# A macaron block on one core: square sums ahead of the splits, a second load queue, and a tile's feed-forward network in the opening stage

## The chip, the cores and the metric

The kernel runs on one NeuronCore of a Trainium2 chip. Five engines work side by side, each in the order of its own instruction list: TensorE (PE; PEld is its weight load), VectorE (DVE), ScalarE (ACT), GpSimd (POOL) and SyncE (SP). DMAs are issued by SP and by ACT, each on its own queue. The metric is the device time of one execution in microseconds (us); lower is better.

## The reference

Two batches of 1024 tokens with 1024 features pass through half a feed-forward network, attention, and the same half feed-forward network again:

```python
def ffn(x):                                   # x: layer norm of the stream
    top2 = softmax over the two largest of x @ gate_w.T       # 8 experts
    low  = x @ lora_A[e].T                    # 16 per expert, 128 together
    return x @ base_w.T + base_b + 2 * sum_e top2[e] * (low[e] @ lora_B[e].T)

def attn(x):                                  # 32 heads of 32, 8 k/v heads
    q, k, v = x @ Wq, x @ Wk, x @ Wv;  q, k = rope(q), rope(k)
    return (softmax(causal(q k^T / sqrt(32))) @ v) @ Wo

x = x + 0.5 * ffn(layernorm(x))
x = x + attn(layernorm(x))
x = x + 0.5 * ffn(layernorm(x))
```

All inputs are fp32.

## The kernel before

**Numbers.** Every fp32 operand of a dense product is kept as a high and a low fp16 part, and a product is three matmuls: high by high, high by low, low by high (`dense`, L362 to L364). Weights must be scaled by a power of two before they are split. `pow2` finds it: ACT squares the whole chunk and adds it up per partition (L170; the squared values themselves go to a place nobody reads, called junk), TensorE spreads the sums over the partitions (L175), POOL takes the square root (L178), and DVE and POOL make the scale and its inverse. `split` then makes both parts of one 128x512 piece: high on ACT (L195) or, for every fourth piece, on POOL (L193), low on DVE (L196).

**Weights.** The gate and lora_A (`prep_gate`), lora_B (`prep_lora`) and the two column blocks of the base matrix (`prep_base`, b0 and b1, eight splits each) stay in SBUF. The attention matrices go as five chunks (2: k and v; 0 and 1: the halves of q; 3 and 4: the halves of the output matrix, called o0 and o1 here) through `prep_stream`: two staged halves are squared, split into two fp16 tiles and written to DRAM (`wstr`), from where the `ws` tiles are later reloaded. Chunks 2, 0 and 1 are also used directly from `ws`. In `prep_stream` junk is the very fp16 tile that the splits then fill, so squares can start only when that tile is free. Staging slots are reused, so a chunk's load is issued when the one before it in the slot has been split.

**Tiles.** Tokens go in 16 tiles of 128. For each: `stage_a1` (layer norm, first ffn in three parts, layer norm again), `stage_a2` (k and v, then both halves of q, rope), attention, `stage_c1` (output matrix), `stage_c2` (second ffn). A layer norm ends with a DMA transpose on SP (`Split.add`, hl to tt, L318). In `ffn` the matmuls of gate and lora_A (24, 128x136) come first, then the two bias adds on POOL (L399), a dozen small operations that pick the experts, and the two halves of 24 matmuls with the three of lora_B each (L444 to L446), added to the stream by DVE (L447).

**The opening.** Up to the first attention unit the order is written by hand: loads on SP, gate, lora_B, b0, b1, then the loop over `START`, in which each entry advances `stage_a1` of that tile by one part and `prep_rest`, the generator of the five chunks, in step; an "f" advances `first_a2`, which runs tiles 0 and 1 together through k/v and q. A scheduler then reorders within the engines by dependences and its own timeline, except where instructions are pinned. The line is

```python
    START = (0, 0, 1, 1, 0, 1, 2, 2, 2, "f", "f", "f", "f", "f", "f")
```

**Attention.** A unit is a tile and a k/v head. L571 makes scores (with a mask matmul, L576), DVE takes the row maximum (L588), writes it beside q, and SP transposes q again (L554); L686 makes scores against that, ACT takes the exponential (L692), POOL masks the diagonal (L694), and L633 multiplies with v. `step(s)` runs the units of tile s and mixes in the dense work that `plan(s)` names; step 0 takes the three parts of tile 3's and of tile 4's `stage_a1`.

Of the kernel before, what the change touches and what calls it, by code (L numbers as in the profile page):

```python
# [9 lines left out]
FP = mybir.dt.float32  # L10
# [29 lines left out]
def kernel(  # L40
# [26 lines left out]
    tp = ctx.enter_context(tc.tile_pool(name="tp", bufs=4))  # L67
# [9 lines left out]
    vp = ctx.enter_context(tc.tile_pool(name="va", bufs=TPB + 1))  # L77
# [31 lines left out]
    kts = stat.tile([P, TPB + 1, NKV, P], HP)  # L109
    wss = [stat.tile([P, 2, KB // 2, 512], HP, name=f"ws{j}") for j in range(3)]  # L110
# [31 lines left out]
    stg = stage_ctx.enter_context(tc.tile_pool(name="stg", bufs=1))  # L142

# [22 lines left out]
    def pow2(aps, junk, name, least=None):  # L166

        am = small.tile([P, 2], FP, name="am")
        for j, (ap, jk) in enumerate(zip(aps, junk)):
            nc.scalar.activation(jk, ap, AF.Square, accum_out=am[:, j : j + 1])  # L170
        sq = small.tile([P, 1], FP, name="sq")
# [6 lines left out]
        nc.gpsimd.tensor_tensor(ar, ar, half, ALU.pow)  # L178
# [11 lines left out]

    def split(hi, lo, src, s, k):
        if k % 4 == 3:
            nc.gpsimd.tensor_scalar(hi, src, s, 0.0, ALU.mult, ALU.add)  # L193
        else:
            nc.scalar.activation(hi, src, AF.Copy, scale=s)  # L195
        nc.vector.scalar_tensor_tensor(lo, src, s, hi, ALU.mult, ALU.subtract)  # L196

    def prep_base(n, sts):
# [6 lines left out]
        pow2(sts, [wb[:, n, 0, h * HK : (h + 1) * HK, :] for h in range(2)], ("b", n), least)  # L205
# [11 lines left out]
    def prep_gate(sts):  # L217
        pow2(sts, [ag[:, 0, h * HK : (h + 1) * HK, :] for h in range(2)], ("a",))
# [7 lines left out]
    def prep_lora(st):  # L226
# [7 lines left out]
        nc.scalar.mul(bb, bb, 0.5)  # L234
# [15 lines left out]
    kth = kth.rearrange("p (a k n) -> p a k n", a=2, n=512)  # L250

    def prep_stream(ci, slots, after, keep):

        parts = CHUNKS[ci][1]
        sts = [staged.pop((ci, h)) for h in range(2)]
        sps = []
        for h in range(2):
            sps.append(wss[slots[h]] if slots[h] < 3 else kth)
            if h == 0:
                for name, c0, c1 in parts:  # L260
                    pow2([st[:, :, c0:c1] for st in sts], [sps[0][:, j, :, c0:c1] for j in range(2)], name)
                    yield
            sp = sps[h]
            for k in range(HK):
                for name, c0, c1 in parts:
                    split(sp[:, 0, k, c0:c1], sp[:, 1, k, c0:c1], sts[h][:, k, c0:c1], S[name], k)
                yield
# [7 lines left out]
    def prep_rest():  # L275
        yield from prep_stream(2, (0, 1), [(1, 0, 0), (1, 1, 1)], True)
        yield from prep_stream(3, (2, 3), [(4, 0, 2), (4, 1, 5)], False)
        yield from prep_stream(0, (2, 0), [None, None], True)
        for j in range(2):
            nc.gpsimd.memset(qst[j][:, :, 3 * DH :], 0.0)  # L280
        yield from prep_stream(1, (1, 2), [None, None], True)
        yield from prep_stream(4, (0, 1), [None, None], False)
# [49 lines left out]
    def layernorm(xt, act=False, n=1):  # L332
# [18 lines left out]
        for i in range(n):  # L351
            c = bass.ts(i, D // n)
            nc.scalar.activation(xn[:, c], xt[:, c], AF.Identity, bias=nb, scale=rs)
# [40 lines left out]
    def ffn(xt, tt, done):  # L394
        psa = p_misc.tile([P, 512], FP, name="misc")
        yield from dense(psa[:, 0 : P + E], tt, lambda k: (ag[:, 0, k, :], ag[:, 1, k, :]))
        for n in range(2):
            c = bass.ts(n, 512)
            nc.gpsimd.tensor_tensor(xt[:, c], xt[:, c], bb[:, c], ALU.add)  # L399
# [26 lines left out]
        yield True  # L426
        psb = [None, None]
# [63 lines left out]
    def kv_out(t, ps):  # L491
        i = t % TPB
        k1 = rope(ps[:, 0:256], 256, NKV, i)
        va = vp.tile([P, NKV, DH], FP, name="va")
# [247 lines left out]


# [15 lines left out]
    a1 = [stage_a1(t) for t in range(3)]  # L759
    next(a1[0])  # L760
    prep_gate(gst)
    pow2([lst[:, bass.ts(h, 512)] for h in range(2)], [lbh[:, bass.ts(h, 512)] for h in range(2)], ("l",))
    b1 = [piece(3 + h, [wb_in[:, 512:1024]], h, nc.sync) for h in range(2)]
    prep_base(0, b0)
    load_x(2)
    next(a1[1])
# [240 lines left out]
```

## Time and profile before

| | |
|---|---|
| median of 3 runs | 1524.11 us (1524.08 to 1530.86) |
| the profiled execution | 1522.65 us |
| its span | 1520.9 us |
| busy: PE, DVE, ACT, POOL | 94%, 70%, 45%, 33% |
| PE busy in the first 152 us | 102.61 us |
| first L686 (start of attention) | 151.96 us |
| DMA | 267.57 MB, mean 176 GB/s |

The page gives busy time per engine and, in 40 equal slices, the busy share in tenths. Matmul ends are modelled, so busy time of PE is not PE at its peak. Lines of the timeline read: start, duration, engine, line, operation, output<-input, count, and in brackets how long the engine had been idle and what ended it. PEclk is the clock granted to TensorE as a share of full speed.

### The profile page before, as it was taken

How to read it: one execution, taken by the hardware profiler on the slowest of the kernel's cores; microseconds unless marked ns; L12 is line 12 of the kernel's file. 1: busy time of each engine (PE TensorE's matmuls, PEld its weight loads, DVE VectorE, ACT ScalarE, POOL GpSimd, SP SyncE). 2: the span in 40 equal slices, each digit the busy share in tenths (PEclk: the TensorE clock that was granted, in tenths of full speed). 3: DMA queues.
4: the chain of work that ended last, by engine and by line, in shares of the span. 5: the costliest groups of instructions: out<-in, count | busy, mean ns of one | idle time of the engine just before them, and what ended most of it. 6: DMA issues, size and time to landing. Idle time of an engine off the chain costs nothing.

```text
span 1520.9 us, 39480 instructions
## 1 busy us (share of the span) xinstructions
PE 1428.8 (94%) x16596; PEld 832.9 (55%) x16596; DVE 1067.4 (70%) x2396; ACT 691.1 (45%) x1280; POOL 496.6 (33%) x711
## 2 busy tenths in 40 slices
PE   3877989899999999999999998999999999999998
PEld 1433445556656566666654454555556566566543
DVE  6978666867768577776663757867777577776653
ACT  7444333544444454454550334444444455565521
POOL 3453342624324133232131423434333132231231
PEclk9998999999999999999999999999999999999999
DMA  9966796957484753646546769668594652663461
GB/s 280 298 195 208 162 276 185 227 152 235 94 249 97 210 173 77 232 118 150 185 119 243 184 163 254 184 183 224 92 269 86 203 169 75 210 143 78 123 190 43
DMA packets 297186, 267.57 MB, mean 176 GB/s; under 512 B 262576, under 2 KB 265648, under 8 KB 276528
## 3 DMA queue, kind: packets, MB, share of 16 engines
q1 hardware_dynamic: 293456, 252.47, 61.4%
q10 hardware_dynamic: 3552, 12.58, 2.2%
q8 instruction: 130, 2.13, 0.6%
q14 instruction: 48, 0.39, 0.1%
HBM read 181.63 MB, written 20.45 MB: 133 GB/s over the span
## 4 chain that ended last, share of the span: by engine, by line
PE 74%; DVE 10%; DMA 8%; issue 2%; POOL 2%; ACT 1%; SPq 1%; DVEq 0%; POOLq 0%; ACTq 0%
PE av L633 15%; PE pd L362 13%; PE pd L363 13%; PE pd L364 13%; PE s L571 8%; PE s L686 7%; DMA ws<-wstr 3%; DMA qt<-qst 3%; DVE ws L196 1%; DVE mx L588 1%; DVE hl L315 1%; DMA tt<-hl 1%; PE pd L444 1%; PE pd L446 1%; PE pd L445 1%
## 5 line engine op out<-in xcount | busy, mean ns | idle before, releaser
L692 ACT ACTIVATE p<-s,cs 128x512 f32<-128x512 f32 x576 | 379.0, 687 | 277.9 <-PE s L686 274.7
L588 DVE TENSOR_REDUCE mx<-s 128x4 f32<-128x512 f32 x480 | 315.8, 675 | 161.7 <-PE s L571 148.7
L633 PE MATMUL av<-p,va 128*32 128x128 f32 x4608 | 236.9, 277 | 1.7 <-POOL p L694 1.0
L362 PE MATMUL pd<-ws,tt 128*128 128x512 f16 x592 | 226.2, 382 | 10.1 <-DMA ws<-wstr 6.3
L633 PE MATMUL av<-p,ones 128*32 128x128 f32 x4608 | 232.2, 273 | 0.0
L363 PE MATMUL pd<-ws,tt 128*128 128x512 f16 x592 | 225.9, 382 | 0.0
L364 PE MATMUL pd<-ws,tt 128*128 128x512 f16 x592 | 225.4, 382 | 0.0
L571 PE MATMUL s<-kts,qt 96*128 96x128 f16 x2304 | 200.0, 220 | 14.1 <-DMA qt<-qst 9.1
L686 PE MATMUL s<-qt,kts 128*128 128x512 f16 x576 | 201.0, 381 | 9.0 <-DMA qt<-qst 6.8
L362 PEld LDWEIGHTS <-tt 128*128 128x128 f16 x1360 | 133.9, 99 | 136.3 <-DMA tt<-hl 13.0
L363 PEld LDWEIGHTS <-tt 128*128 128x128 f16 x1360 | 133.9, 98 | 132.1 <-issue 15.2
L571 PEld LDWEIGHTS <-qt 96*128 96x128 f16 x2304 | 151.4, 98 | 98.3 <-issue 35.7
L364 PEld LDWEIGHTS <-tt 128*128 128x128 f16 x1360 | 134.0, 99 | 127.8 <-issue 6.5
L362 PE MATMUL pd<-wb,tt 128*128 128x512 f16 x512 | 196.0, 383 | 7.7 <-DMA tt<-hl 3.7
L363 PE MATMUL pd<-wb,tt 128*128 128x512 f16 x512 | 195.5, 382 | 1.0 <-DVE wb L196 1.0
L364 PE MATMUL pd<-wb,tt 128*128 128x512 f16 x512 | 195.3, 381 | 0.0
L633 PEld LDWEIGHTS av<-p,va 128*32 128x32 f32 x4608 | 122.5, 110 | 68.6 <-issue 59.4
L642 DVE RECIPROCAL rc<-o 128x128 f32<-128x128 f32 x128 | 121.0, 945 | 49.8 <-ACT o L640 49.6
L649 POOL TENSOR_TENSOR tt<-o,tt 128x128 f16<-128x128 f32 x128 | 55.5, 434 | 295.6 <-ACT tt L648 295.5
L694 POOL TENSOR_SCALAR_AFFINE_SELECT p<-p 128x512 f32<-128x512 f32 x128 | 84.3, 659 | 200.9 <-ACT p L692 200.9
L633 PEld LDWEIGHTS av<-p,ones 128*32 128x32 f32 x4608 | 138.3, 110 | 0.1
L583 POOL TENSOR_SCALAR_AFFINE_SELECT sm<-sm 128x512 f32<-128x512 f32 x96 | 62.1, 647 | 204.2 <-ACT sm L582 203.9
(175 smaller groups left out, 1796.0 us busy)
## 6 DMA issues: line engine op xcount, KB each, us to landing
ws<-wstr SPq DMA_DIRECT2D x148, 1024.0 KB, 5.6
wstr<-ws ACTq DMA_DIRECT2D x9, 1024.0 KB, 5.6
xt<-in_x_dram SPq DMA_DIRECT2D x16, 512.0 KB, 4.2
out_dram<-xt SPq DMA_DIRECT2D x15, 512.0 KB, 2.9
qt<-qst SPq DMA_TRANSPOSE x256, 3.2
ws<-in_wb_dram SPq DMA_DIRECT2D x2, 1024.0 KB, 8.3
qst<-in_wb_dram SPq DMA_DIRECT2D x2, 1024.0 KB, 7.3
st<-in_wo_dram SPq DMA_DIRECT2D x2, 1024.0 KB, 10.0
```

The costliest lines, as they stand in the source:

```text
L362: nc.tensor.matmul(ps, lhsT=th, rhs=wh, start=(k == 0), stop=False)
L363: nc.tensor.matmul(ps, lhsT=th, rhs=wl, start=False, stop=False)
L364: nc.tensor.matmul(ps, lhsT=tl, rhs=wh, start=False, stop=(last and k == KB - 1))
L571: nc.tensor.matmul(ps[:, h, :], lhsT=q[0 : 3 * DH, h, :], rhs=KT[b0 + j][0 : 3 * DH, g, :], start=(not pem or h == 0), stop=not pem,)
L583: nc.gpsimd.affine_select(out=sm, in_=sm, compare_op=ALU.is_ge, fill=-3.0e38, base=0, pattern=[[0, GRP], [-1, P]], channel_multiplier=1,)
L588: nc.vector.tensor_reduce(mx[:, j, :], ps, AX.X, ALU.max)
L633: prev = nc.tensor.matmul(av[rows, i, :], lhsT=w, rhs=p32[:, h, :], start=(us[0][0] == 0 and n == 0 and i == 0), stop=(us[-1][0] == L - 1 ...
L642: nc.vector.reciprocal(rc, o[:, 1, :])
L649: nc.gpsimd.tensor_tensor(c.low(g), o2, c.high(g), ALU.subtract)
L686: ins = nc.tensor.matmul(ps.rearrange("p h k -> p (h k)"), lhsT=KT[b0 + j][:, g, :], rhs=q.rearrange("p h k -> p (h k)"), start=True, stop ...
L692: nc.scalar.activation(p32, ps, AF.Exp, scale=cs)
L694: nc.gpsimd.affine_select(out=p32, in_=p32, compare_op=ALU.is_ge, fill=0.0, base=0, pattern=[[0, GRP], [1, P]], channel_multiplier=-1,)
```

## The change

Six things, all in the opening or in what it touches:

- Squares and the rest of `pow2` are separate. `stream_squares` squares the next chunk into a junk tile of its own after the second step of the current chunk's first half, and not ahead of the last ACT split of b1. `base_squares` and the gate's squares are called apart from `pow2` likewise: b0's squares are named before those of lora_B.
- b1 and the k/v chunk are loaded through ACT's queue, behind tile 0's normalised copy (`xn`); before, b1 went through SP's queue and k/v through ACT's, later.
- The bias is loaded and halved earlier, and the two bias adds of a tile move behind the expert choice and behind the last `pow2` power on POOL.
- `START` runs tile 0 and then tile 1, and takes tile 3's three parts between the "f" entries; step 0 keeps tile 4's only. Tile 4's input load moves there too.
- The v tiles become one tile `vas` with ten places (nine before); the last eight hold the first half of o0 during the opening, so o0 no longer goes through `ws` tile 2.
- The pool of tt tiles has five buffers (four before).

```diff
-    tp = ctx.enter_context(tc.tile_pool(name="tp", bufs=4))
+    tp = ctx.enter_context(tc.tile_pool(name="tp", bufs=5))
-    vp = ctx.enter_context(tc.tile_pool(name="va", bufs=TPB + 1))
+    vas = stat.tile([P, TPB + 2, NKV, DH], FP)
+    junk = stg.tile([P, 1, HK, 512], HP, name="junk").to_broadcast([P, 2, HK, 512])
-    def pow2(aps, junk, name, least=None):
+    def squares(aps, junk):
         am = small.tile([P, 2], FP, name="am")
         for j, (ap, jk) in enumerate(zip(aps, junk)):
             nc.scalar.activation(jk, ap, AF.Square, accum_out=am[:, j : j + 1])
+        return am
+    def pow2(am, name, least=None):
...
-        nc.gpsimd.tensor_tensor(ar, ar, half, ALU.pow)
+        marks["pow"] = nc.gpsimd.tensor_tensor(ar, ar, half, ALU.pow)
...
+    def stream_squares(ci):
+        if (ci, 0) not in staged or (ci, 1) not in staged or ci in sums:
+            return
+        sts = [staged[ci, h] for h in range(2)]
+        with tc.issue_after(marks["b1"].ins):
+            sums[ci] = [
+                squares([st[:, :, c0:c1] for st in sts], [junk[:, j, :, 0 : c1 - c0] for j in range(2)])
+                for _, c0, c1 in CHUNKS[ci][1]
+            ]
-    def prep_stream(ci, slots, after, keep):
+    def prep_stream(ci, slots, after, keep, nxt):
...
+                if k == 1 and nxt is not None:
+                    stream_squares(nxt)
...
-        yield from prep_stream(3, (2, 3), [(4, 0, 2), (4, 1, 5)], False)
+        yield from prep_stream(3, (4, 3), [(4, 0, 2), (4, 1, 5)], False, 0)
...
     def ffn(xt, tt, done):
-        for n in range(2):
-            c = bass.ts(n, 512)
-            nc.gpsimd.tensor_tensor(xt[:, c], xt[:, c], bb[:, c], ALU.add)
...
         yield True
+        with tc.issue_after(marks["pow"].ins):
+            for n in range(2):
+                c = bass.ts(n, 512)
+                nc.gpsimd.tensor_tensor(xt[:, c], xt[:, c], bb[:, c], ALU.add)
...
-    a1 = [stage_a1(t) for t in range(3)]
+    a1 = [stage_a1(t) for t in range(4)]
     next(a1[0])
+    with tc.issue_after(marks["xn"].ins):
+        b1 = [piece(3 + h, [wb_in[:, 512:1024]], h, nc.scalar) for h in range(2)]
+        stage(2, 0, 0, nc.scalar)
+        stage(2, 1, 1, nc.scalar)
     prep_gate(gst)
-    pow2([lst[:, bass.ts(h, 512)] for h in range(2)], [lbh[:, bass.ts(h, 512)] for h in range(2)], ("l",))
-    b1 = [piece(3 + h, [wb_in[:, 512:1024]], h, nc.sync) for h in range(2)]
-    prep_base(0, b0)
+    am = base_squares(0, b0)
+    pow2(squares([lst[:, bass.ts(h, 512)] for h in range(2)], [lbh[:, bass.ts(h, 512)] for h in range(2)]), ("l",))
+    prep_base(0, b0, am)
+    marks["b0"] = marks[2]
     load_x(2)
-    next(a1[1])
     pin(nc.sync.dma_start(out=bb, in_=bias_in.partition_broadcast(P)))
-    stage(2, 0, 0, nc.scalar)
-    stage(2, 1, 1, nc.scalar)
-    prep_base(1, b1)
+    nc.scalar.mul(bb, bb, 0.5)
+    for _ in chunk(a1[0]):
+        pass
+    with tc.issue_after(marks["b0"].ins):
+        am = base_squares(1, b1)
+    next(a1[1])
+    prep_base(1, b1, am)
+    marks["b1"] = marks[6]
...
     load_x(3)
+    load_x(4)
...
-    START = (0, 0, 1, 1, 0, 1, 2, 2, 2, "f", "f", "f", "f", "f", "f")
+    START = (0, 0, 1, 1, 1, 2, 2, 2, "f", "f", 3, "f", 3, "f", 3, "f", "f")
...
         if s == 0:
-            return [("a1", 3)] * 3 + [("a1", 4)] * 3
+            return [("a1", 4)] * 3
```

## The prediction, before the changed kernel ran

> **What bounds the kernel now.** I read the busy slices of the page first, then busy time by stretch, then the list of TensorE's instructions with the idle time before each, then the same list of the other engines up to the first attention unit.
>
> ```profile
> PE   3877989899999999999999998999999999999998
> PEclk9998999999999999999999999999999999999999
> ```
>
> ```profile
> 0.00:152.00 152.00, 102.61 (x511) 50.32 (x512) 119.15 (x293) 82.69 (x130) 66.96 (x101) 0.91 0.80 245
> 152.00:180.00 28.00, 27.25 (x211) 13.06 (x210) 19.61 (x53) 10.37 (x22) 10.20 (x18) 1.00 0.64 174
> 180.00:260.00 80.00, 71.04 (x698) 37.50 (x702) 52.59 (x128) 29.90 (x63) 24.62 (x39) 0.98 0.84 213
> 260.00:500.00 240.00, 233.69 (x2847) 140.26 (x2836) 182.69 (x404) 113.18 (x216) 90.12 (x125) 0.99 0.68 177
> ```
>
> Columns: stretch, its length, busy time (instructions) of PE, PEld, DVE, ACT, POOL, then granted clock, DMA share, GB/s. TensorE is the bound from the first attention unit on (27.25 of 28 us, 233.69 of 240). Only the first four slices have holes: 49.4 us of the first 152 are idle (152 - 102.61), at a mean clock of 0.91. That is the stage the change rewrites.
>
> ```profile
> 35.97 0.61 PE L362 MATMUL pd<-wb,tt 128*128 128x512 f16 x1 [3.67 <-DMA tt<-hl]
> 85.90 0.80 PE L175 MATMUL s<-ident,sq 128*128 128x128 f32 x2 [6.25 <-DVE sq L173]
> 110.02 0.38 PE L542 MATMUL pd<-ws,tt 128*128 128x512 f16 x1 [2.79 <-ACT va L495]
> 124.24 0.79 PE L175 MATMUL s<-ident,sq 128*128 128x128 f32 x2 [8.13 <-DVE sq L173]
> 151.96 0.38 PE L686 MATMUL s<-qt,kts 128*128 128x512 f16 x1 [0.61 <-DMA qt<-qst]
> ```
>
> The two longest holes stand before L175, the matmul that spreads a chunk's sum of squares: TensorE works in order, and that matmul waits for squares that come late. The last line is the first L686, the start of attention for tile 0; I use it as the clock of this stage: 151.96.
>
> ```profile
> 79.17 1.90 ACT L170 ACTIVATE ws<-qst 128x2048 f16<-128x2048 f32 x1
> 89.27 1.93 ACT L195 ACTIVATE ws<-qst,s_q 128x512 f16<-128x512 f32 x3
> 41.76 8.77 POOL L399 TENSOR_TENSOR xt<-xt,bb 128x512 f32<-128x512 f32 x6 [4.03 <-ACT bb L234]
> 23.36 2.61 ACTq L158 DMA_DIRECT2D st<-in_wv_dram  x1
> 17.68 1.53 SPq L158 DMA_DIRECT2D qst<-in_wb_dram  x2
> ```
>
> Squares of the first q chunk start at 79.17 (behind tile 2's lh, 77.86) and its splits only at 89.27. POOL's six bias adds (1.46 us each) hold back the k and v power until 50.5. The second base block is issued at 17.68, after tile 0's transpose. The fourth DMA that ACT issues in a row takes 2.61 us.
>
> **The change part by part.** Counts do not change: the same squares, splits, bias adds, matmuls. So the sum is a sum of shifts, read from the two instruction orders with the durations above.
>
> *b1 and k/v loads on ACT's queue.* They now stand behind tile 0's xn and hl and ahead of the gate splits (11.20 before). xn ends near 10.15 (its nb is ready at 8.9). Six issues follow: the trace has 0.44, 0.86, 0.54 and 2.61 for the four k/v loads (512 KB each), and b1's two of 1 MB come ahead of them; the sixth also waits until the second half of b0 has landed (issued 4.8, median 8.3 to landing: 13.1). Free again at 13.7 if nothing is held, at 19.8 if three issues cost 2.61; I take two, 17.3, as the 2.61 row is the nearest. Gate splits +6.1. The squares of lora_B (1.25 us) now lie between b0's squares: +1.25. b0's splits start near 28.5 (21.3).
>
> Against that, b1 (2 MB) is there early. The Trainium skill ("DMA: Bandwidth & Descriptors", section "Issuing engines are not separate DMA queues") speaks against this part: DMAs of all issuing engines interleave on the same 16 engines, and only the sequencer's issue time is saved. The trace shows DMA nearly idle (share 0.06) from 14.25 to 16.5, before tile 0's transpose moves, so the gain would be an earlier start and not bandwidth. By the rule b0's rest is slowed while both queues run, which the 13.7 to 19.8 contains. By this trace the early b1 is worth nothing in the sum: b1's squares must wait for ACT's b0 splits (28.5 + 3.9), as they did before.
>
> *b1's splits.* Squares end at 36.5. POOL's power stands behind tile 2's hl, and DVE's tile 0 add behind two bias adds (2.9): splits at 46.6 to 52.8, before 35.2 to 44.0. +9.
>
> *Bias adds in pairs behind the power; squares ahead.* The power of k and v no longer waits behind 8.8 us of adds. ACT after b1's splits (46.6 + 6 x 0.63 = 50.4, less waiting than DVE): lora_B's part is done by 51, though k/v's four squares (1.15 each) end near 54, o0's two (2.0 each) near 57.5, half of q0's near 59.6, since all of them stand ahead of the k/v splits. These then run on DVE 59.6 to 66.3 (16 of 0.39 and small ones; before 53.9 to 62.3): +4. DVE goes on when q0's second square is in (66.7): eight o0 splits of 0.66, tile 1's two adds 1.4, one hl 1.2, two statistics 1.2, about 14 small ones 2.3: 78 (72.4). q0's first half then needs no new square: small ones 1.5, four splits with two small ones 3.2: 79 to 83, where it was 90.0 to 94.7. This is where the change pays: 11 us.
>
> *The a2 stage of tiles 0 and 1.* TensorE is in order: tile 2's L446 comes first and needs its ll, which DVE does behind q0's splits. k/v of tile 0 start at 84.7 (86.87), 7.5 us with the cold clock. The square matmul of o1 now stands ahead of tile 1's k/v: ACT does it after tile 0's outputs (0.36 + 0.37 + 1.24 + 2.09), so tile 1's k/v run 97.3 to 104.3 (99.6 before). From here nothing late is left in front of TensorE: q0 48 x 0.2155 = 10.3, tile 3's network 13.2 (24 x 0.059, 54 x 0.2155, one transpose), two score units 2.2, q1 10.3: 36.0. First L686 at 140.3, 11.7 earlier. (Before, the same 36 us took 52.4: holes of 1.3, 2.8, 8.1 and 0.6, some 2.2 of cold clock, 1.2 of tile 4's gate.)
>
> *Tile 3's network moved.* The trace already shows it ahead of 151.96 (gate from 106.2, the rest up to 149.8), put there by the scheduler. So the move brings no new filler into the holes; it fixes the place. Its two layer norms, two transposes on SP and 12 gate operations on DVE go with it, in the same gaps.
>
> *What is late next.* In the new order the first four units (L686, L571, L633) follow each other without dense work between, since tile 4's transpose on SP waits behind theirs. Each unit must go through exp (0.69), the POOL mask (0.66), max (0.68) and a transpose DMA (3.2): 7.4 us of matmuls in up to 14 us. No row of before shows this; 2 to 9 us bound it, I take 5. Here the second rule: "TensorE: Matmul & The Clock Gate", section "What's actually happening", says that an idle window of about 3.4 us halves the clock, until about as long of work. The trace agrees: after the 8.13 us hole the granted clock is 0.50 and L362 comes every 0.427 us instead of 0.2155. By the trace's rows alone these units cost 5; by the rule a 4 us wait among them adds 1.7, which I leave to the range. Tile 4's gate (20 x 0.06 = 1.2) is not yet done. Later, of the 9 us idle in 180 to 260, 5.3 are waits for ws, qt and tt at 179 to 194; with more units finished beforehand I count 3 as covered, 0 to 5 possible.
>
> A fifth tt buffer and the vas tile: the order from about 285 us on is the same on TensorE, so nothing.
>
> Sum: -11.7 + 5 + 1.2 - 3 = -8.5. The profiled execution took 1522.65 (span 1520.9 and 1.75 around it): 1514.1. The median of three, 1524.11, is 1.5 above it, so 1515.5 for the median.
>
> **Rivals.** *Given back:* the first four units cost 9 and nothing is covered later: -11.7 + 9 + 1.2 = -1.5, 1522.5. For it: the kernel is at TensorE's bound from 152 on, and the move adds no filler. Against: the 8.13 hole is real work time regained. That the move does nothing belongs here.
>
> *Slower:* ACT is held by its six issues to 19.8 or later (+2.5), and the 16 splits of q0, q1 and o1 run beside POOL's hl and bias adds. The four at 99.06 beside such adds took 5.97 us, 1.49 each, against 0.73 alone; eight of those add 6. First L686 at 149, and the four units cost 9 and 1.7 of cold clock: -3 + 10.7 + 1.2 = +9, 1533. It decides from a first L686 later than about 146. For it: base block 0 and 1 come 7 and 9 us later in my own sum, and everything on ACT is serial. Against: DVE has 33 us idle in the first 152.
>
> **How the numbers follow.** About 0.5% (7.6 us) is what a measurement of this kernel can tell from no change. Forecast (1505 to 1517) 0.47; given back (1517 to 1529) 0.22; slower 0.31. With chances of both signs the range must reach both: ACT free at 13.7 and 2 us in the units give 1508, more cover later 1503; the slower case reaches past 1535 with a chance near 0.15. Range 1503 to 1535; the forecast's own is the 1505 to 1517 above. Faster 0.47, same 0.22, slower 0.31.
>
> **What would show it.** Right: gate splits on ACT near 17; b1 splits near 47; q0's first splits near 79 to 83; no hole over 3 us before the square matmuls after 100; first L686 near 140; 5 us idle in the next 15. Wrong: gate splits after 20, tile 1's k/v ending past 108, or the first L686 past 146 (slower); the four units with over 8 us idle (given back).

## The result and the profile after

The changed kernel takes **1528.51 us** (median of 20 runs, 1524.77 to 1535.11), the kernel before beside it 1523.80 (median of 20, 1519.71 to 1530.86). The ratio is 1.003, with a 95% interval of 1.0021 to 1.004: slower by 0.3%. Forecast was 1515.5. The profiled execution took 1530.01 us, its span 1528.2. Line numbers shift: L175 is now L180, L195 and L196 are L202 and L203, L315 and L318 are L341 and L344, L362 is L388, L399 is L453, L542 is L569, L571 is L598, L633 is L660, L686 is L713, L694 is L721.

The busy slices of the page, then busy time by stretch (columns as in the prediction: PE, PEld, DVE, ACT, POOL, granted clock, DMA share, GB/s):

```profile
PE   2879898899999999999999998999999999999998
PEclk9989799999999999999999999999999999999999
```

```profile
0.00:152.00 152.00, 105.09 (x502) 51.21 (x502) 112.17 (x293) 84.67 (x131) 61.39 (x100) 0.93 0.75 232
152.00:180.00 28.00, 19.73 (x148) 10.80 (x148) 19.97 (x44) 7.54 (x18) 11.27 (x15) 0.64 0.66 173
180.00:260.00 80.00, 72.58 (x686) 39.50 (x685) 55.58 (x128) 29.24 (x62) 28.08 (x41) 0.98 0.82 216
```

In the first stretch TensorE is busy 2.5 us longer. The second, where before had 27.25 of 28 us busy at full clock, has 19.73 at a clock of 0.64. The fifth slice is where PEclk dips to 7.

To place the whole loss I take the second issue of a finished tile to the output: 319.92 us before, 327.29 after, 7.37 later. The same stretches around that point, first before, then after:

```profile
0.00:319.92 319.92, 254.50 (x2035) 132.72 (x2035) 237.09 (x571) 150.36 (x270) 129.52 (x194) 0.94 0.79 219
319.92:1520.90 1200.98, 1174.31 (x14562) 700.13 (x14561) 830.34 (x1826) 540.75 (x1011) 367.13 (x517) 1.00 0.60 164
```

```profile
0.00:327.29 327.29, 259.76 (x2036) 137.66 (x2036) 239.18 (x571) 152.33 (x270) 130.02 (x194) 0.93 0.76 214
327.29:1528.20 1200.91, 1173.05 (x14562) 699.37 (x14561) 829.95 (x1826) 541.46 (x1011) 368.43 (x517) 1.00 0.61 164
```

The remainder is equal (1200.98 and 1200.91), so everything lies ahead of that point, with the same TensorE work (2035 and 2036 recorded matmuls). Of the 7.37 us, TensorE was idle for 2.11 more (67.53 against 65.42) and busy for 5.26 more: the same matmuls ran at a lower clock (0.93 against 0.94 over the stretch). This point (called *second output* below) is the yardstick for all runs.

TensorE's instructions with the idle time before each, the lines that answer to those of before:

```profile
86.29 0.49 PE L180 MATMUL s<-ident,sq 128*128 128x128 f32 x2 [0.61 <-DVE s_q L191]
104.99 0.79 PE L180 MATMUL s<-ident,sq 128*128 128x128 f32 x2 [4.90 <-DVE sq L178]
148.11 0.38 PE L713 MATMUL s<-qt,kts 128*128 128x512 f16 x1
...
153.52 0.66 PE L660 MATMUL av<-p,vas 128*32 128x128 f32 x8 [3.93 <-POOL p L721]
159.04 0.65 PE L660 MATMUL av<-p,vas 128*32 128x128 f32 x8 [4.43 <-POOL p L721]
...
163.21 0.66 PE L660 MATMUL av<-p,vas 128*32 128x128 f32 x8 [1.68 <-POOL p L721]
```

The two holes before square matmuls shrank (6.25 to 0.61, 8.13 to 4.90; a third, of 3.33, now stands at 72.79), but the first score matmul of tile 0 against the maximum (L713; *first score* below) came only 3.85 us earlier, at 148.11 against a forecast of 140.3, and then four waits for POOL's mask (3.93, 4.43, 1.68 and a last one of 0.64) cost 10.68 us. Busy time by finer stretches shows the clock there:

```profile
152.00:160.00 8.00, 2.04 (x32) 1.18 (x32) 8.00 (x10) 1.44 (x3) 6.98 (x7) 0.50 0.97 292
160.00:172.00 12.00, 9.68 (x77) 5.80 (x74) 8.71 (x24) 4.45 (x12) 3.01 (x6) 0.50 0.58 109
```

From 152 to 172 the 11.72 us of matmuls ran at half the clock, which costs half of them, 5.9 us. That is about the 5.26 above.

### The profile page after: what moved, and what is told of

Read it like the earlier page. It is cut to its first block, busy times and chain, and to the rows that moved or that the text cites. A ratio compares the mean times of both kernels' runs of the same rounds, so it can differ in the third digit from the quotient of the medians.

```text
span 1528.2 us, 39477 instructions
## 1 busy us (share of the span) xinstructions
PE 1432.8 (94%) x16596; PEld 837.0 (55%) x16596; DVE 1069.1 (70%) x2396; ACT 693.8 (45%) x1280; POOL 498.4 (33%) x711
## 3 DMA queue, kind: packets, MB, share of 16 engines
HBM read 181.63 MB, written 20.45 MB: 132 GB/s over the span
## 4 chain that ended last, share of the span: by engine, by line
PE 76%; DVE 8%; DMA 7%; POOL 3%; issue 3%; ACT 1%; SPq 1%; ACTq 0%; DVEq 0%; POOLq 0%
PE av L660 15%; PE pd L388 13%; PE pd L389 13%; PE pd L390 13%; PE s L598 8%; PE s L713 7%; DMA ws<-wstr 3%; DMA qt<-qst 2%; DVE mx L615 1%; DVE hl L341 1%; DMA st<-in_wk_dram 1%; PE misc L388 1%; DMA tt<-hl 1%; PE misc L389 1%; PE misc L390 1%
## 5 line engine op out<-in xcount | busy, mean ns | idle before, releaser
L660 PE MATMUL av<-p,vas 128*32 128x128 f32 x4608 | 237.7, 278 | 13.6 <-POOL p L721 13.4
L388 PE MATMUL pd<-ws,tt 128*128 128x512 f16 x592 | 225.0, 380 | 10.3 <-DMA ws<-wstr 7.2
L660 PE MATMUL av<-p,ones 128*32 128x128 f32 x4608 | 233.2, 274 | 0.0
L598 PE MATMUL s<-kts,qt 96*128 96x128 f16 x2304 | 199.3, 220 | 14.1 <-DMA qt<-qst 11.1
L713 PE MATMUL s<-qt,kts 128*128 128x512 f16 x576 | 201.3, 381 | 5.0 <-DMA qt<-qst 2.9
L388 PEld LDWEIGHTS <-tt 128*128 128x128 f16 x1360 | 135.1, 99 | 128.9 <-issue 6.4
L598 PEld LDWEIGHTS <-qt 96*128 96x128 f16 x2304 | 151.2, 98 | 98.7 <-issue 33.0
L388 PE MATMUL pd<-wb,tt 128*128 128x512 f16 x512 | 196.4, 384 | 2.9 <-ACT wb L202 1.4
L660 PEld LDWEIGHTS av<-p,vas 128*32 128x32 f32 x4608 | 122.6, 110 | 79.7 <-issue 55.5
L721 POOL TENSOR_SCALAR_AFFINE_SELECT p<-p 128x512 f32<-128x512 f32 x128 | 87.2, 681 | 211.2 <-ACT p L719 210.9
L660 PEld LDWEIGHTS av<-p,ones 128*32 128x32 f32 x4608 | 138.9, 111 | 0.2
```

Of the source, the lines that this page charges most:

```text
L388: nc.tensor.matmul(ps, lhsT=th, rhs=wh, start=(k == 0), stop=False)
L598: nc.tensor.matmul(ps[:, h, :], lhsT=q[0 : 3 * DH, h, :], rhs=KT[b0 + j][0 : 3 * DH, g, :], start=(not pem or h == 0), stop=not pem,)
L660: prev = nc.tensor.matmul(av[rows, i, :], lhsT=w, rhs=p32[:, h, :], start=(us[0][0] == 0 and n == 0 and i == 0), stop=(us[-1][0] == L - 1 ...
L713: ins = nc.tensor.matmul(ps.rearrange("p h k -> p (h k)"), lhsT=KT[b0 + j][:, g, :], rhs=q.rearrange("p h k -> p (h k)"), start=True, stop ...
L721: nc.gpsimd.affine_select(out=p32, in_=p32, compare_op=ALU.is_ge, fill=0.0, base=0, pattern=[[0, GRP], [1, P]], channel_multiplier=-1,)
```

## Where the front got late

The lists of ACT (ACTq: its DMA issues) and of SP's queue, after. Before, the gate splits started at 11.20, tile 0's transpose took SP from 15.57 for 2.06 us, and the gate matmuls began at 20.00.

```profile
10.26 1.03 ACTq L159 DMA_DIRECT2D qst<-in_wb_dram  x2
11.32 0.57 ACTq L159 DMA_DIRECT2D st<-in_wk_dram  x1
11.92 3.72 ACTq L159 DMA_DIRECT2D st<-in_wv_dram  x1
15.68 2.88 ACTq L159 DMA_DIRECT2D st<-in_wk_dram  x1
18.60 1.85 ACTq L159 DMA_DIRECT2D st<-in_wv_dram  x1
20.50 1.39 ACT L202 ACTIVATE ag<-ws,s_a 128x544 f16<-128x544 f32 x2 [9.20 <-issue]
```

```profile
12.58 6.87 SPq L344 DMA_TRANSPOSE tt<-hl  x1
```

Two things happen at once. The last three issues take 3.72, 2.88 and 1.85 us, and ACT computes nothing for 9.2 us. And the small transpose needs 6.87 us to leave SP: from 14 to 16 us the DMA engines, which before were nearly idle there, are now full. Busy time by stretch, after:

```profile
14.00:16.00 2.00, 0.00 (x0) 0.00 (x0) 0.00 (x0) 0.00 (x0) 0.00 (x0) 1.00 1.03 397
```

(397 GB/s; before, 0.12 and 49.) With no transposed tile and no gate splits, no compute engine has work there. The gate matmuls begin at 27.92. Which of the two was last there? TensorE's list, then the landing of tile 0's transpose (the longest of the two in the first 40 us):

```profile
27.34 0.80 PE L180 MATMUL s<-ident,sq 128*128 128x128 f32 x2 [1.00 <-DVE sq L178]
27.92 0.32 PE L388 MATMUL misc<-ag,tt 128*128 128x136 f16 x1
```

```profile
DMA to landing us min/median/max: 4.3/9.2/14.0
```

The transpose landed at 26.6 (12.58 + 14.0). The gate matmuls did not wait for it: they follow the square matmul of b0 without a gap, and that one waited for ACT's squares. So in this kernel the held ACT was the later of the two, by about 1.3 us.

## Experiments

Each ratio is to the kernel before, run beside it on the same chip; second output and first score are from the one profiled execution (before: 319.92 and 151.96; after: 327.29 and 148.11). "Loads" are the six early issues on ACT's queue, "plan" is tile 3's network moved into `START`, "squares" the square sums ahead, "adds" the bias adds behind the power.

| kernel | ratio (95%) | first score | second output |
|---|---|---|---|
| e1: after, plan back | 1.0023 (1.0010 to 1.0037) | 155.04 | 327.31 |
| e2: after, loads back | 0.9971 (0.9955 to 0.9987) | 140.62 | 316.91 |
| e3: after, adds back | 1.0122 (1.0097 to 1.0147) | 161.72 | 346.08 |
| e4: before, plan moved | 1.0103 (1.0074 to 1.0133) | 159.70 | 338.56 |
| e5: after, k/v's loads back, b1's not | 1.0057 (1.0036 to 1.0077) | 139.65 | 325.67 |
| e6: after, loads behind the gate splits | 1.0032 (1.0017 to 1.0047) | 143.48 | 327.75 |
| e7: after, tile 4's adds later | 1.0020 (1.0010 to 1.0029) | 148.56 | 327.65 |
| e8: after, loads and plan back | 0.9942 (0.9924 to 0.9960) | 143.97 | 312.50 |
| e9: e8, adds back | 1.0087 (1.0065 to 1.0109) | 161.92 | 333.20 |
| e10: before, adds moved | 1.0042 (1.0026 to 1.0058) | 157.59 | 332.74 |
| e11: e8 with b1 loaded early | 0.9965 (0.9953 to 0.9978) | 148.58 | 320.64 |
| e12: e8 with four tt buffers | 0.9988 (0.9975 to 1.0001) | 147.50 | 318.76 |
| e13: after, loads on POOL's queue | 1.0067 (1.0051 to 1.0083) | 150.33 | 331.24 |
| e14: e13, plan back | 1.0044 (1.0027 to 1.0061) | 156.08 | 327.98 |
| e15: after, leaves out tile 0 to 3's adds | 1.0101 (1.0081 to 1.0121) | 148.87 | 337.27 |
| e16: e8, ACT held instead of loads | 1.0019 (1.0004 to 1.0033) | 154.72 | 326.67 |
| e17: e8, loads on POOL at ACT's time | 1.0031 (1.0017 to 1.0044) | 154.26 | 328.76 |

### e1 to e4: which part loses

Theory: the late front loses it. Rivals: tile 3's network is the filler that the first units then lack, or the bias adds stand in front of the masks.

```diff
# e2: the six loads at their old places and queues
-    with tc.issue_after(marks["xn"].ins):
-        b1 = [piece(3 + h, [wb_in[:, 512:1024]], h, nc.scalar) for h in range(2)]
-        stage(2, 0, 0, nc.scalar)
-        stage(2, 1, 1, nc.scalar)
     prep_gate(gst)
...
+    b1 = [piece(3 + h, [wb_in[:, 512:1024]], h, nc.sync) for h in range(2)]
     prep_base(0, b0, am)
...
     next(a1[1])
+    stage(2, 0, 0, nc.scalar)
+    stage(2, 1, 1, nc.scalar)
# e1: the plan back (e4 is the reverse of it, in the kernel before)
-    START = (0, 0, 1, 1, 1, 2, 2, 2, "f", "f", 3, "f", 3, "f", 3, "f", "f")
+    START = (0, 0, 1, 1, 1, 2, 2, 2, "f", "f", "f", "f", "f", "f")
-            return [("a1", 4)] * 3
+            return [("a1", 3)] * 3 + [("a1", 4)] * 3
# e3: the two adds of a tile at their old place, ahead of the gate's result
```

> The changed kernel with its new preparation of weights, but tile 3's feed-forward network and the load of tile 4 back in step 0 of the plan, as before the change. Theory 'no filler': the loss stands in the first four attention units, where TensorE has no dense work between score and attention-value matmuls and waits 10.7 us for POOL's masks, the clock at half speed until about 172. Then this kernel has those waits down to 3 us or less and a clock of 1.0 there, its first L713-type score matmul near 148, and it takes 1515 to 1520 us. Theory 'late front': the loss is that ACT's six loads stand in front of the gate splits (20.5 us instead of 11.2) and the base blocks come late; the plan does not touch that, so this kernel stays at 1526 to 1530.

> The changed kernel with the loads of the second base block back on SP behind tile 0's transpose and of k and v on ACT behind the second norm, so that no load stands in front of the gate splits. Both theories: gate splits start near 11 to 12 instead of 20.5. Theory 'late front': this is handed on, the first score matmul of tile 0 comes 5 us or more earlier than 148.1, and the time falls by 4 us or more, to 1524 or less. Theory 'no filler': what is won at the front is eaten by waits for loads and by the serial split work up to 90, and the four units keep their 10 us of waits: 1526 to 1531.

> The changed kernel with the bias adds of the feed-forward network back ahead of the gate work, not behind the power on POOL. In the changed kernel tile 4's two adds (2.96 us) stand right in front of the second unit's mask on POOL, whose lateness makes a 4.43 us wait. Theory 'adds in front of the mask': the four units wait 7 to 8 us instead of 10.7, and the time falls by 3 to 4 us, unless the power of k and v at the front is held back again as in the kernel before (8.8 us of adds at 41.8), which would give 3 to 5 us back. Theory 'no filler': the four units keep 8 us or more of waits, time 1525 to 1531.

> The kernel before with only the move: tile 3's feed-forward network placed by hand in the beginning, tile 4's load ahead of it, and step 0 left with tile 4's first stage alone; squares, bias adds and loads as before. Theory 'no filler': the four first units wait 6 to 11 us with the clock at half speed, and the kernel is 5 to 12 us slower than the one before, 1529 to 1536. Theory 'late front': the move costs nothing, 1522 to 1526.

**e2** is the clearest: faster than before, and the first score at 140.62, as forecast for the whole change (140.3). Its gate splits start at 11.08. SP's queue, then TensorE around the first units:

```profile
12.46 3.08 SPq L344 DMA_TRANSPOSE tt<-hl  x1
```

```profile
140.62 0.59 PE L713 MATMUL s<-qt,kts 128*128 128x512 f16 x2
147.52 0.66 PE L660 MATMUL av<-p,vas 128*32 128x128 f32 x8 [6.30 <-POOL p L721]
```

The six loads alone cost 7.5 us at the first score and 10.4 at the second output. The mask wait is there too (6.30), so it is not theirs. **e1** has no mask wait, so the filler rival has a real effect; but the time lost before the first score takes its place. SP's queue shows why its first score is late: three weight loads, which wait 11.1 us for the weights to be written to DRAM (`wstr`), stand ahead of the transposes of q, though DVE had their input ready at 145.0.

```profile
136.75 12.63 SPq L400 DMA_DIRECT2D ws<-wstr  x3
149.44 14.68 SPq L581 DMA_TRANSPOSE qt<-qst  x8
```

e1 and after end within 0.07% of each other: in this front the plan is worth nothing either way. **e3** refutes the adds as the loss: with them at the old place the changed kernel is 0.9% worse, with three holes of 6.59, 9.28 and 6.30 us between 86 and 115. **e4**, the plan in the kernel before with four tt buffers, is 1.0% slower: TensorE waits 18.63 us in one piece. Its first scores are done at 141, but DVE writes their maxima beside q only at 151.38, behind o1's splits, rope and a layer norm's hl; the transposes of q leave right then, SP having been free since 149.49.

```profile
151.38 0.24 DVE L599 SCALAR_TENSOR_TENSOR qst<-mx,qst 128x4 f16<-128x4 f32 x2
```

```profile
151.57 7.37 SPq L554 DMA_TRANSPOSE qt<-qst  x4
```

```profile
159.70 0.59 PE L686 MATMUL s<-qt,kts 128*128 128x512 f16 x1 [18.63 <-DMA qt<-qst]
```

### e5 to e8: which loads, where, and the mask waits

```diff
# e5: only k/v's two stage(2, ...) lines back; b1's stay
# e6: the six loads behind the gate splits
-    with tc.issue_after(marks["xn"].ins):
+    prep_gate(gst)
+    with tc.issue_after(marks[0].ins):
...
-    prep_gate(gst)
# e7: tile 4's adds wait for the second mask
-                nc.gpsimd.affine_select(
+                m = nc.gpsimd.affine_select(
...
+                if t == 0 and g < 2:
+                    marks["pow"] = m
# e8: e1 and e2 together (squares, adds and the fifth tt remain)
```

> The changed kernel with only the four loads of k and v moved back behind the second norm on ACT; the two loads of the second base block stay on ACT's queue in front of the gate splits. Theory 'the later loads of the row are held': in the changed kernel's trace the issues take 1.03 for the base block's two together and then 0.57, 3.72, 2.88 and 1.85 us, so without the last four ACT is free at about 11.3, gate splits start near 11.5, base block 0's splits near 24 to 25, the first score matmul of tile 0 near 140, and the time is near that of the kernel with all six moved back: 1519 to 1524. Theory 'the base block's own loads hold ACT or slow base block 0 by sharing the DMA engines': base block 0 comes 3 us or more later than in the kernel with all six moved back, time 1525 or more.

> The changed kernel with all six loads behind the gate splits on ACT instead of in front of them; they are still in front of base block 0's squares. If what counts is the gate splits, this kernel is as fast as the one with all six moved back (1519 to 1524). If what counts is base block 0 (squares, power, splits), which still stands behind 8 to 10 us of issues, it stays where the changed kernel is: base block 0's splits near 31, first score matmul near 147 to 149, 1526 to 1530.

> The changed kernel with only tile 4's two bias adds moved on POOL behind the second attention mask (they stood in front of it). Theory 'adds in front of the mask': the wait in front of the second attention-value matmul falls from 4.43 to about 1.5 us and the time by 2 to 4 us, to 1525 or less. Rival 'DVE and SP are late as well': in that stretch DVE is busy without a gap for 10 us and the next query transposes leave at 156.6, so the wait only moves to the next unit: 1527 to 1530.

> The changed kernel with all six loads moved back and also tile 3's network back in step 0. Left of the change: squares ahead into the junk tile, bias adds behind the power, five tt buffers. Theory 'the move costs nothing with this front': within 3 us of the kernel with only the loads moved back (1522.2), since what tile 3's network fills between units stood as filler before the first unit. Theory 'filler pays': the first score matmul of tile 0 near 146 with no wait over 3 us in the next 20 us, time 1514 to 1518.

**e5** was to regain a good part; it lost. Its first score is the earliest of all (139.65), yet its second output (325.67) is 8.8 us behind e2's: four bare units with waits of 2.76 and 5.37 us for the mask ran at a clock of 0.60 (139 to 160). So an early first score is not a good stage by itself. (The profiled execution, 1528.01, is the shortest of e5's seven, whose median is 1534.63; its lines show less than the loss in the ratio.) **e6** frees the gate splits (11.07) and the first score (143.48), but the six issues still hold ACT ahead of b0's squares: b0's splits still come at 30.23, and one mask wait is 7.37. There is no gain at the end.

**e7** tests the second mask wait. POOL's list of after has two reasons for the waits:

```profile
151.45 0.73 POOL L505 TENSOR_TENSOR t<-qs,sinT 128x256 f32<-128x256 f32 x1 [2.43 <-DVE t L513]
...
152.82 0.65 POOL L721 TENSOR_SCALAR_AFFINE_SELECT p<-p 128x512 f32<-128x512 f32 x1
153.44 1.04 POOL L340 TENSOR_SCALAR hl<-xn 128x1024 f16<-128x1024 f32 x1
154.45 2.96 POOL L453 TENSOR_TENSOR xt<-xt,bb 128x512 f32<-128x512 f32 x2
157.37 1.62 POOL L721 TENSOR_SCALAR_AFFINE_SELECT p<-p 128x512 f32<-128x512 f32 x1
```

The first mask stands behind rope products that wait for DVE (8.00 of 8 us busy from 152 to 160), the second behind tile 4's hl and adds (4.00 us). With the adds later the second wait fell from 4.43 to 0.97, and waits of 2.33, 0.76 and 1.93 took its place: 10.55 us in all, for 10.68. The rival, that the wait only moves, holds.

**e8** beats both kernels: 1517.19, 0.58% faster than before (interval 0.40 to 0.76%), and nothing waits in the first units until 179.62. Busy time of its second stretch:

```profile
152.00:180.00 28.00, 26.66 (x212) 12.96 (x210) 21.32 (x62) 9.95 (x22) 9.89 (x18) 1.00 0.66 147
```

So squares and adds with the fifth tt buffer are a gain (e8 also keeps the small rest of the change: o0's own place, the earlier bias, tile 0 before tile 1). The loads undo it and more. The plan, worth nothing beside the loads, seems to cost 0.3% without them (e2 against e8; the intervals overlap by a hair).

### e9 to e12: what is inside the gain of e8

```diff
# e9: e8 with the adds at their old place; e10: the kernel before with this alone
+        marks["pow"] = nc.gpsimd.tensor_tensor(ar, ar, half, ALU.pow)
...
+        with tc.issue_after(marks["pow"].ins):
+            for n in range(2):
...
# e11: e8, but b1's two loads early on ACT
# e12: e8 with four tt buffers
-    tp = ctx.enter_context(tc.tile_pool(name="tp", bufs=5))
+    tp = ctx.enter_context(tc.tile_pool(name="tp", bufs=4))
```

> Of the change only the squares ahead into the junk tile and the fifth tt buffer are left; loads, plan and bias adds are as before the change. If the gain of the kernel with loads and plan moved back (0.9942 of before) comes from the squares, this one stands at 0.994 to 0.997 (1517 to 1522). If it comes from the bias adds (POOL's power of k and v not held back by 8.8 us of adds), this one stands at 0.999 or above, since the squares then still wait for that power: k and v splits near 54 as before, and the long waits in front of the square matmuls replaced by waits of the same length for splits.

> The kernel before with only the bias adds moved behind the power. If the adds are the gain, 0.994 to 0.997 (1517 to 1522): POOL's power of k and v comes 8 us earlier and with it the k and v splits and all that follows. If the squares are the gain, the 6.25 and 8.13 us waits in front of the square matmuls stay, and the time is within 2 us of before. If each needs the other, both this run and the squares alone are at 0.998 to 1.002 though the two together give 0.994.

> The kernel with loads of k and v and the plan moved back, but with the second base block's two loads still on ACT's queue in front of the gate splits. With the move in place the early base block came out slower (1.0057) although its first score matmul was 1 us earlier, with four bare units in front of the dense work and half the clock. If that was the four units, then with tile 3's network back between the units the early base block is as fast as or faster than the kernel without it: 1513 to 1518. If the two early loads do harm at the front (tile 0's transpose on SP takes 6.05 us to leave instead of 3.08), it is 3 us or more slower than that: 1520 or more.

> The kernel with loads and plan moved back, with four tt buffers instead of five. If the fifth buffer is nothing, as forecast (the order from 285 us on is the same on TensorE), the same 1517 within 2 us. If a transpose has to wait for a free tt in the first 250 us, 3 us or more slower, with TensorE waiting for tt in the trace where it did not.

Squares ahead (with the fifth buffer and e8's small rest) without the adds: +0.87%. The adds without the squares: +0.42%. Both: -0.58%. Each alone leaves or makes holes elsewhere. In e9 b1's splits are at 43.89, and TensorE has holes of 8.61, 6.71 and 6.42 us. In e10 one transpose is late, as its layer norm is (POOL waited 3.05 us for ACT's xn):

```profile
117.14 0.29 PE L364 MATMUL misc<-ag,tt 128*128 128x136 f16 x1 [7.81 <-DMA tt<-hl]
```

e11 prices b1's early load at +0.23% (the intervals overlap), and k/v's on top of it at +0.58% (e1 against e11). e12 prices the fifth buffer at 0.46%. SP's queue in e12: tile 3's transpose, whose hl was ready at 112.5, leaves only at 130.34 (in e8 at 112.80), weight loads follow, and only then the transposes of q (in e8 they leave at 138.26).

```profile
130.34 1.70 SPq L344 DMA_TRANSPOSE tt<-hl  x1
132.20 7.50 SPq L400 DMA_DIRECT2D ws<-wstr  x3
139.75 20.94 SPq L581 DMA_TRANSPOSE qt<-qst  x8
```

### e13 to e17: ACT's time or the DMA engines

An issue on ACT costs ACT's time and fills the DMA engines. Which of them loses?

```diff
# e13: the six loads on another queue (e14: with the plan back)
-        b1 = [piece(3 + h, [wb_in[:, 512:1024]], h, nc.scalar) for h in range(2)]
-        stage(2, 0, 0, nc.scalar)
-        stage(2, 1, 1, nc.scalar)
+        b1 = [piece(3 + h, [wb_in[:, 512:1024]], h, nc.gpsimd) for h in range(2)]
+        stage(2, 0, 0, nc.gpsimd)
+        stage(2, 1, 1, nc.gpsimd)
# e17: as e14, but behind the gate's power on POOL, the time at which ACT issued
+    with tc.issue_after(marks["pow"].ins):
# e16: e8, ACT kept busy behind tile 0's hl, gate splits and squares behind it
+        for _ in range(9):
+            marks["held"] = nc.scalar.activation(
+                junk[:, 0, 0:2], xts[0].rearrange("p (k n) -> p k n", n=512), AF.Copy
+            )
# e15: bias adds from the fifth network on only
```

> The changed kernel with the same six early loads, issued from POOL's queue instead of ACT's. If what harms is that ACT is held, the base block 0 squares start near 11 to 13 and its splits near 24, the first score matmul comes near 140 to 142 and the time is that of the kernel with the loads moved back (1519 to 1524), though POOL is held instead until about 20 and the gate's power with it. If what harms is the sharing of DMA engines (base block 0's second half and tile 0's transpose land late), base block 0's splits stay at 28 or later and the time at 1526 or more.

> As the run before, with tile 3's network back in step 0. Held ACT as the cause: near the kernel with loads and plan moved back (0.994 of before), 1514 to 1519. Sharing as the cause: near the kernel with the loads on ACT and the plan back (1.002 of before), 1526 to 1531.

> The changed kernel without the bias adds of tiles 0 to 3 (left out of the computation; tile 4's stay). If POOL's adds beside DVE's splits stretch them, the o0 splits end 3 to 4 us earlier than 85.5, tile 0's k and v start 3 to 4 us earlier than 92.5, the first score matmul near 144 to 145, and the time falls by 3 to 4 us, to 1524 to 1526. If the stretch is only waiting that something else would cause, k and v of tile 0 start within 1 us of 92.5 and the time stays at 1527 to 1530.

> The kernel with loads and plan moved back, with nine extra activations (tile 0's x into the junk tile, about 1 us each) on ACT where the six issues stood in the changed kernel, between tile 0's hl and the gate splits: ACT is held for about 9 us, the DMA engines are not. Held ACT as the cause: gate splits near 20, base block 0's splits near 31 to 33, and the time near that of the kernel with the loads on ACT and the plan back (1.002), 1526 to 1531. Sharing as the cause: 0.994 to 0.997, 1516 to 1521.

> The changed kernel with the plan back and the six loads on POOL's queue behind the gate's power (about 10.5 us, when ACT issued them in the changed kernel) instead of behind the first statistics (6.6 us). Held ACT as the cause: base block 0's splits near 24 to 26 and the time 0.994 to 0.997, 1516 to 1521. Sharing as the cause: tile 0's transpose takes 6 us or more to leave SP, its gate matmuls start at 26 or later, and the time stays at 1.002 or above, 1526 to 1532.

e13 and e14 issued earlier than the changed kernel (6.62 us), which also delayed b0's second half (ACT waited 4.01 us for it), so they do not separate the two. In e16 and e17 each cause stands alone. In e16 ACT is held until 21.71 by arithmetic, DMA is free, and the transpose leaves in 3.10 us:

```profile
11.07 8.66 ACT L797 ACTIVATE junk<-xt 128x1024 f16<-128x1024 f32 x8
```

In e17 ACT is free (gate splits at 11.10, b0's at 21.32), the loads start when they do in after (11.13 for 10.26, but all six are out at 15.83 for 20.45), and the transpose takes 11.71 us. POOL's time for the issues held nothing visible: b0's splits came earlier than in e2 (24.55) and e8 (25.77). SP's queue, TensorE and ACT of e17:

```profile
12.48 11.71 SPq L344 DMA_TRANSPOSE tt<-hl  x1
```

```profile
29.73 0.29 PE L388 MATMUL misc<-ag,tt 128*128 128x136 f16 x1 [11.01 <-DMA tt<-hl]
```

```profile
32.73 0.27 ACT L425 ACTIVATE lg<-misc,cg 128x8 f32<-128x8 f32 x1 [4.82 <-PE misc L390]
```

This is where the branches meet: ACT stands 4.82 us for the late gate matmuls, ahead of its next work, the second square of b1.

| plan back in all four | DMA free | loads early |
|---|---|---|
| ACT free | 0.9942 (e8) | 1.0031 (e17) |
| ACT held | 1.0019 (e16) | 1.0023 (e1) |

Each cause can lose the 0.8 to 0.9% by itself, in the size that it has here. But both sizes are larger than in e1, and so the table does not say how much of the loss is which. Tile 0's k/v matmuls show it: 85.56 in e8, 91.44 in e1, 97.28 in e16 and 96.01 in e17. e16 brings b0's splits at 35.10 (30.42 in e1), and e17's transpose lands at 29.7 (26.3 in e1). That e1 still has the same first score, 155.04, is due to the weight loads in its SP queue above. What is shown is that there are two branches to one meeting point, ACT's gate and base splits on one side, tile 0's transpose and gate matmuls on the other, and that the later one sets the stage. In after the two are about 1.3 us apart: with ACT free and all 4 MB still in flight, the transpose would have let the gate matmuls start only that much earlier. Taking away a part of the load helps both: with the plan back, b1's 2 MB alone early (e11) cost 0.23%, all six 0.81% (e1).

**e15** tests the stretching of DVE's splits beside POOL's adds (next section); it leaves tile 0 to 3's adds out of the computation. The durations answered (o0's splits at 0.74 us and hl at 1.21, beside no adds); the time did not, because ACT's order changed and ACT waited 6.83 us for q's load in front of o0's splits, which ended at 90.3. What the stretching alone costs at the end stays open.

## Why the prediction was wrong

Forecast: -8.5 us from the profiled execution. Measured: +7.4. Of these 15.9 us, 7.8 were missing at the first score (148.11 for 140.3) and 8.1 came behind it. The "slower" rival described what came: gate splits late, splits beside POOL's adds, four units with 10.7 us of waiting and cold clock. It put its point of decision at a first score of about 146; it came at 148.11. Two more of the signs for "wrong" were there: gate splits after 20, and tile 1's k/v ending at 113.3, past 108. That 1528.51 lies inside the range of 1503 to 1535 says little, as the range was drawn to hold both signs.

**Step "b1 and k/v loads on ACT's queue": mis-sized, and a part of its price left out.** Gate splits were forecast at 17.3 with bounds of 13.7 and 19.8; they came at 20.50, outside. Two expensive issues at 2.61 were counted; there were three, of 3.72, 2.88 and 1.85. (On the basis of its own bounds two come to 17.8, not 17.3.) This term went on through all later ones; the times of splits are ACT's first, but for the end of o0's, which is DVE's:

| step | before | forecast | after | e2 (loads back) |
|---|---|---|---|---|
| gate splits | 11.20 | 17.3 | 20.50 | 11.08 |
| b0's splits | 21.3 | 28.5 | 31.48 | 24.55 |
| b1's splits | 36.35 | 46.6 | 47.81 | 36.73 |
| k/v splits (ACT) | 53.4 | 59.6 | 62.97 | 55.87 |
| end of o0's splits | 72.4 | 78 | 85.5 | 76.2 |
| tile 0's k/v matmuls | 86.87 | 84.7 | 92.50 | 84.86 |
| first score | 151.96 | 140.3 | 148.11 | 140.62 |

e2 puts a number on the whole term: without the six early loads the first score comes 7.5 us earlier and the second output 10.4.

**Step "the trace shows DMA nearly idle from 14.25 to 16.5".** It took an idle gap as room. With the loads there, tile 0's transpose took 6.87 us to leave SP, for 2.06 before and 3.08 in e2. The section "Issuing engines are not separate DMA queues" of the Trainium skill ("DMA: Bandwidth & Descriptors") spoke against this part, and the prediction weighed it for the rest of b0 only. Filled engines alone are not the mark: in e2 their share was 1.12 from 12.5 to 15.5, filled by the loads issued before it, and the transpose left in 3.08. What differs is the 4 MB more. In after the transpose stayed just hidden behind the held ACT; e17 shows that it can cost 0.9% with ACT's time not touched at all, though at a transpose 4.8 us longer than after's. How the loss in after divides between the two stays open.

**Step "DVE goes on ... eight o0 splits of 0.66": a mis-sized term.** o0's stage ended 7.5 us after its forecast (85.5 for 78), 4.6 of it carried over from the front (the stage began at 71.33, not 66.7), 2.9 new. DVE's and POOL's lists of after:

```profile
71.33 1.21 DVE L177 TENSOR_TENSOR sq<-am 128x1 f32<-128x1 f32 x1
...
76.92 2.44 DVE L203 SCALAR_TENSOR_TENSOR vas<-st,s_o,vas 128x512 f16<-128x512 f32 x2
79.29 2.28 DVE L341 TENSOR_TENSOR hl<-xn,hl 128x1024 f16<-128x1024 f32 x1
81.63 0.74 DVE L203 SCALAR_TENSOR_TENSOR kts<-kts,s_o 128x512 f16<-128x512 f32 x1
...
85.84 0.13 DVE L177 TENSOR_TENSOR sq<-am 128x1 f32<-128x1 f32 x1
```

```profile
71.00 2.76 POOL L453 TENSOR_TENSOR xt<-xt,bb 128x512 f32<-128x512 f32 x2
...
77.48 3.01 POOL L453 TENSOR_TENSOR xt<-xt,bb 128x512 f32<-128x512 f32 x2
```

Beside the adds a split takes 1.22 instead of 0.74, hl 2.28 instead of 1.21, and a sum of one element per partition 1.21 instead of 0.13. Those four instructions are 1.08 + 2 x 0.48 + 1.07 = 3.1 us too long, about the 2.9. The Trainium skill ("SBUF — State Buffer", section "SBUF: two separate sides") says that a DVE instruction with two SBUF inputs and a GpSimd instruction that reads SBUF exclude each other for the whole instruction. The rows agree: that 1.21 is about one add (2.76 / 2 = 1.38). The adds were not new in number, but this change put them beside these splits.

Little of these 2.9 us can have reached q0's splits, forecast at 79 and come at 86.33 on ACT and 87.74 on DVE, for ACT was late as well. The prediction had q0's first half in "need no new square"; but the squares of the next chunk, q1, stand ahead of q0's splits in ACT's list, and ACT waits there for q1's load:

```profile
83.27 1.91 ACT L171 ACTIVATE junk<-st 128x2048 f16<-128x2048 f32 x1 [4.36 <-DMA st<-in_wq_dram]
...
86.33 1.95 ACT L202 ACTIVATE ws<-qst,s_q 128x512 f16<-128x512 f32 x3 [1.07 <-DVE s_q L191]
```

With DVE on time, ACT could have started these splits 1.07 us earlier and no more. In e2 they stand ahead of that square, at 71.85.

**Step "what is late next": right in its kind, too small.** Forecast 5 us of waiting among the four bare units (bounds 2 to 9) and no cold clock; measured 10.68 and 5.9. The rule of "TensorE: Matmul & The Clock Gate", section "What's actually happening", that an idle window halves the clock, was priced at 1.7 and left to the range. The trace says more than one window: from 152, in the 3.93 us hole, the clock was 0.50 until 172, as further waits followed. The order on POOL could be read beforehand from the program; the sum did not count the adds and rope products that stand ahead of the masks. That DVE is full there was not seen.

**Step "a fifth tt buffer ... nothing": wrong.** It is worth 0.46% (e12 against e8). The buffer works earlier than the 285 us that the step looked at, in SP's queue.

**What held.** The two longest holes before square matmuls shrank, though one was 4.90 where the sign for "right" was none over 3. From tile 1's k/v (about 113) to the first score there was no hole, 34.8 us for 36.0 forecast. The move gained no time (e1 against after). Cover after 180: idle time 7.42 for 8.96 up to 260, 4.93 for 6.31 from there to the second output, 2.9 us for the 3 forecast. And the part that the prediction valued, squares with adds, does gain: 0.58%, about 9 us, in e8. One reading was off without bearing on the sum: the page's sixth and eighth slices stand at 8 too, so the first four are not the only ones with holes.

## What to carry to other kernels

An idle gap of the DMA engines in front of a small transfer that everything waits for is not free room, and an issuing engine's time is part of a load's price. When both are hit, mending one may show little, so undo the whole load before judging the parts. A stand-in for one cause must have the size of the original: here both were larger, so they show what can happen and not each share. Pieces of a reordering need not be additive (squares +0.87%, adds +0.42%, both -0.58%): leave single parts out of the whole, besides adding them alone. Before a stage is left with little dense work, list what stands ahead of its smallest link on each engine, here the mask on POOL, and price the cold clock with the wait.

## What the runs showed of the hardware

- The issue of one small DMA transpose (tile 0's) held SP for 2.06 and 3.08 us with no bulk weight load issued behind b0's, and for 6.87, 11.71, 13.10 and 14.41 us with six more in flight (before, e2, after, e17, e13, e14).
- DMA issues on ACT took about 0.5 us each at first and 1.85 to 3.72 from the fourth on (after); the same loads on POOL's queue took 0.75 each for the four of 512 KB (e13, e17), without growing.
- A sum of one element per partition on DVE took 1.21 us beside POOL's adds and 0.13 without (after, 71.33 and 85.84).
